# A 12-stage decoder on one core: hand-ordered mixture loop in layer 0, and a context LayerNorm in four steps

## Chip, cores and metric

One core of one Trainium2 chip runs the whole program. The metric is the device time of one execution in microseconds. Before the change it is 1590.72 us, the median of three runs.

## What is computed

A decoder of four layers, each with self-attention, cross-attention to a context and a feed-forward part, on 4 batches of 256 tokens with 128 features. Two pieces matter here: the cross-attention of layer 0 and the feed-forward part of layer 0.

```python
x = x + _L0_attn_ref(_layernorm(x), ...)
x = x + _L0_xattn_ref(_layernorm(x), ctx_1024, mask_BxS2_bk0, ...)
x = x + _L0_ffn_ref(_layernorm(x), L0_ffn_gate_w, shared..., routed...)   # 32 experts, the best one taken
...
def _L2_xattn_ref(features, masks, latents, gm, bm, ...):
    x = _layernorm(features, gm, bm)          # features = ctx_1024
    ...
```

In `_L0_ffn_ref` each of the 1024 tokens goes to one of 32 experts (hidden size 256), `silu(x @ gate) * (x @ up) @ down`, and a shared expert of the same form is added. The LayerNorm of the context, 4 x 512 rows, is needed in layer 2, but the kernel computes it while layer 0 runs.

## The kernel before

**Where the order of work comes from.** The program is written in Python order, and the framework then puts each engine's instructions into a fixed queue. Unless told otherwise it chooses that queue itself, in a simulated run made before the launch: when an engine is free in the simulation it takes, among the instructions whose inputs and buffers are ready, the one written first. An instruction written much later can so be pulled forward into a gap. [...] `tc.manual_schedule(engines=...)` makes the queues of the named engines follow the written order inside its block.

**The mixture loop (`mixture`, called from `ffn0`).** Tokens are sorted by expert into 16 blocks of 128 rows, each made of four groups of 32 rows (`per` = 32, `m` = 4); a group belongs to one expert. For block `b`:

- `fetch(b)`, L1053: GpSimd (POOL) gathers the 128 rows by an indirect DMA into `xb`, six buffers, five blocks ahead.
- `rows_T(b)`: PE turns `xb` (L1060) into a bank of tag `t`, and ACT copies it to `xbT` (L1062).
- `weights_in(b)`, L1034: DVE copies the four experts' first weights, 128x512 each, from the resident `e0h` to `wbh`, two buffers. The column offsets are read into DVE registers from the table `at`.
- `hidden(b)`: eight matmuls (L1075, two for each group of 32 rows), then ACT's Silu `sg` (L1173), then DVE's product `h` (L1174).
- `turned(b)`: PE turns `h` by two transposes (L1084) into a bank of tag `t`, and DVE copies it to `hT` (L1086).
- `weights_out(b)`, L1039: ACT copies the four experts' second weights, 128x256 each, from `e0d` to `wbd`, three buffers.
- `result(b)`: sixteen matmuls (L1096) into `y`; after every fourth block ACT copies `y` to `ys` (L1109) and SP's queue stores it to `done` (L1110).

The tag `t` has two PSUM banks, shared by `rows_T` and `turned`. An iteration of the loop (L1121 on) holds the steps of neighbouring blocks: `weights_in(b+1)`, `weights_out(b)`, `hidden(b)`, `rows_T(b+1)`, `fetch(b+5)`, `turned(b-1)`, `result(b-2)`. After the loop, layer 1 loads `w1x` through SP's queue and starts with matmuls on it (L1309). The same function serves layers 1 and 2 with `per` = 128; those have no weight copies.

**The context LayerNorm (`normalise_context`, L1984).** Layer 0's attention is woven by hand out of eight units, four for self-attention and then four for cross-attention; each unit has a list `beside` of extra steps, spread evenly over its length. A cross unit of batch `b` has two such steps, and each normalises two 128-row tiles of `cn` in place: `statistics` makes mean and variance on DVE (L287, L288) and the reciprocal root on POOL (L293, L295, the power -0.5); `scaled_by` then applies them on DVE (L301). POOL also computes the attention's own LayerNorm scaling (`xn`, L301) and adds a bias row to `x` (L347). DVE's main work in the units is the row maximum `mx` (L477), which reads PSUM banks of tag `s1` that PE fills.

Of the kernel before, what the change touches and what calls it, by code (L numbers as in the profile page):

```python
# [10 lines left out]

# [1 line left out]

# [1 line left out]

# [15 lines left out]
P = 128  # L33
# [3 lines left out]
NKT = SK // P  # L37
# [146 lines left out]
def decoder(ctx: ExitStack, tc: tile.TileContext, dr, out):  # L184
    nc = tc.nc
    V, A, G, T = nc.vector, nc.scalar, nc.gpsimd, nc.tensor
# [11 lines left out]
    def ps(tag):  # L198
        cols = 1024 if tag == "sc" else 512
        return psum[0].tile([P, cols], F32, tag=tag, name=tag, bufs=BANKS.get(tag, 2))  # L200

    @contextmanager
    def psum_pool(name):
        with tc.tile_pool(name=name, bufs=2, space=PSUM, reuse_waits="tile") as psum[0]:
            yield
# [19 lines left out]
    cn = const.tile([P, B * NKT, D], F32, tag="cn", name="cn")  # L225
# [49 lines left out]
    def normalise(srcs, dsts, on=None):  # L275

        scaled_by(statistics(srcs), srcs, dsts, on)

    def statistics(srcs, twice=False):

        n = len(srcs)
        mv = small.tile([P, 2, 2], F32, tag="mv", name="mv")
        for i, s in enumerate(srcs):
            st = small.tile([P, 6], F32, tag="st", name="st")
            V.bn_stats(st, s)  # L287
            V.bn_aggr(mv[:, i, :], st)  # L288
        ve = small.tile([P, 2], F32, tag="ve", name="ve")
        if twice:  # L290
            G.tensor_scalar(ve[:, :n], mv[:, :n, 1], 1.0 + EPS, EPS * EPS, ALU.mult, ALU.add)
        else:
            G.tensor_scalar(ve[:, :n], mv[:, :n, 1], EPS, None, ALU.add)  # L293
        rs = small.tile([P, 2], F32, tag="rs", name="rs")
        G.tensor_tensor(rs[:, :n], ve[:, :n], halves[:, :n], ALU.pow)  # L295
        return mv, rs

    def scaled_by(stats, srcs, dsts, on=None):
        mv, rs = stats
        for i, (s, d) in enumerate(zip(srcs, dsts)):  # L300
            (on or V).tensor_scalar(  # L301
                d, s, mv[:, i, 0:1], rs[:, i : i + 1], ALU.subtract, ALU.mult
            )
# [70 lines left out]
    def call(f, *args):  # L374
        return lambda *more: f(*args, *more)
# [362 lines left out]
    def turned(xn, pool):  # L738
        xnT = pool.tile([P, S], F32, tag="xnT", name="xnT", bufs=3)
        transposed(xn, xnT, tag="s1")  # L740
        return xnT
# [255 lines left out]
    def mixture(pool, n_e, per, hots, weights, rows_, wh, wd, activate, biases=None):  # L997
# [7 lines left out]
        m = P // per  # L1005
        size = -(-(k * NT * m + n_e - 1) // m)
        tiles_ = [slice(j * per, (j + 1) * per) for j in range(m)]
        n1, n2 = wh.shape[1] // n_e, wd.shape[1] // n_e
# [8 lines left out]
        xb, xbT, h, hT, y = {}, {}, {}, {}, {}  # L1017
        ahead = 5

        def offsets(i, b, engine):  # L1020

            _, values = nc.values_load_multi_w_load_instructions(
                at[0:1, b, i, :], engines=[engine], min_val=0, max_val=(n_e - 1) * widths[i],
                skip_runtime_bounds_check_because="an expert's number, limited to the last one's",
            )
            return values
# [3 lines left out]
        def weights_in(b):  # L1030

            w = wb[0, b] = pool.tile([P, m, n1], F32, tag="wbh", name="wbh", bufs=2)
            for j, v in enumerate(offsets(0, b, mybir.EngineType.DVE)):
                V.tensor_copy(w[:, j, :], wh[:, bass.ds(v, n1)])  # L1034

        def weights_out(b):
            w = wb[1, b] = pool.tile([P, m, n2], F32, tag="wbd", name="wbd", bufs=3)
            for j, v in enumerate(offsets(1, b, mybir.EngineType.Activation)):
                A.copy(w[:, j, :], wd[:, bass.ds(v, n2)])  # L1039

        def taken(i, b, n):

# [8 lines left out]
        def fetch(b):  # L1051
            xb[b] = pool.tile([P, D], F32, tag="xb", name="xb", bufs=ahead + 1)
            G.indirect_dma_start(  # L1053
                out=xb[b], out_offset=None, in_=sent[:, :],
                in_offset=bass.IndirectOffsetOnAxis(ap=token[:, b : b + 1], axis=0),
            )

        def rows_T(b):
            tp = ps("t")[:, :P]
            T.transpose(tp, xb[b], ident)  # L1060
            xbT[b] = pool.tile([P, P], F32, tag="xbT", name="xbT", bufs=3)
            A.copy(xbT[b], tp)  # L1062

        def hidden(b):
            o = [ps("g") for _ in range(0, n1, 512)]
            blocks = taken(0, b, 512)
            for i, p in enumerate(o):
                if biases is not None:
                    (at_h,) = offsets(0, b, mybir.EngineType.PE)
                    T.matmul(  # L1070
                        p, lhsT=onesb[0:3, :], rhs=biases[0:3, bass.ds(at_h, 512)],
                        start=True, stop=False,
                    )
                for r, w in blocks:
                    T.matmul(  # L1075
                        p[r], lhsT=xbT[b][:, r], rhs=w(512 * i), start=biases is None, stop=True,
                    )
            h[b] = pool.tile([P, n2], F32, tag="h", name="h", bufs=3)
            activate(pool, h[b], o)

        def turned(b):
            tp = ps("t")
            for i in range(nh):
                T.transpose(tp[:, i * P : (i + 1) * P], h[b][:, i * P : (i + 1) * P], ident)  # L1084
            hT[b] = pool.tile([P, n2], F32, tag="hT", name="hT", bufs=3)
            V.tensor_copy(hT[b], tp[:, :n2])  # L1086

        def result(b):
            g, i = b // 4, b % 4
            if i == 0:  # L1090
                y[g] = ps("y")
            cols = slice(i * P, (i + 1) * P)
            blocks = taken(1, b, P)
            for c in range(nh):
                for r, w in blocks:
                    T.matmul(  # L1096
                        y[g][r, cols], lhsT=hT[b][:, c * P : (c + 1) * P][:, r], rhs=w(c * P),
                        start=c == 0, stop=c == nh - 1 and biases is None,
                    )
            if biases is not None:  # L1100
                (at_b,) = offsets(2, b, mybir.EngineType.PE)
                T.matmul(
                    y[g][:, cols], lhsT=onesb[0:3, :],
                    rhs=biases[0:3, bass.ds(at_b + n_e * n1, P)], start=False, stop=True,
                )
            if b == groups[g][-1]:
                n = len(groups[g])
                ys = pool.tile([P, 4, D], F32, tag="ys", name="ys")
                A.copy(ys[:, :n, :], y[g][:, : n * P].rearrange("p (n d) -> p n d", n=n))  # L1109
                nc.sync.dma_start(  # L1110
                    done[4 * g * P : (4 * g + n) * P, :].rearrange("(n p) d -> p n d", p=P),
                    ys[:, :n, :],
                )
# [4 lines left out]
        if per < P:  # L1118
            weights_in(0)
        rows_T(0)  # L1120
        for b in range(size + 2):  # L1121
            if per < P and b + 1 < size:
                weights_in(b + 1)
            if per < P and b < size:
                weights_out(b)
            if b < size:
                hidden(b)
            if b + 1 < size:
                rows_T(b + 1)
            if b + ahead < size:  # L1130
                fetch(b + ahead)
            if 1 <= b <= size:
                turned(b - 1)
            if b >= 2:
                result(b - 2)

        def bring(b):
            out = []
# [842 lines left out]

    def normalise_context(b, i):  # L1984
        two = [cn[:, NKT * b + i, :], cn[:, NKT * b + i + 1, :]]
        normalise(two, two)

    def turn_context(b):
        tp = ps("s1")
# [16 lines left out]
    def layer_0(wh):  # L2006
        with ExitStack() as st:
            st.enter_context(psum_pool("ps0"))
            pool = attn_pool(st, "l0")
            neg0, neg0T = key_mask(pool, "mbk0", False)  # L2010
            for i in range(0, 32, 4):
                cols = slice(i * 512, (i + 4) * 512)
                nc.sync.dma_start(wh[:, cols], dr["e0h"][:, cols])
            units = self_units(pool, w0a, True, False, 0)
            units += cross_units(
                pool, w0x, 2, context_T,
                row_mask=lambda b: neg0[:, b * SK : (b + 1) * SK],
                key_bias=lambda b: lambda kt: neg0T[:, NKT * b + kt : NKT * b + kt + 1],
            )
            for u in units[B:]:  # L2020
                u.beside = [call(normalise_context, u.b, i) for i in range(0, NKT, 2)]
            woven(pool, units, SK)

    def layer_1(w, loads):
# [38 lines left out]
    with tc.tile_pool(name="e1", bufs=1, reuse_waits="tile") as experts:  # L2063
        w1x = load("w1x", pool=late, on=nc.sync)

        def loads():
# [6 lines left out]
        ahead = right.enter_context(  # L2073
            tc.tile_pool(name="ahead", bufs=1, side="right", reuse_waits="tile")
        )
# [27 lines left out]
```

## Time and profile before

| what | value |
|---|---|
| median of three runs | 1590.72 us (1585.98 to 1591.83) |
| profiled execution, own time | 1587.75 us |
| its span, first to last instruction | 1586.0 us |
| PE busy | 1351.7 us (85%) |
| DVE / ACT / POOL busy | 824.2 / 726.2 / 277.9 us |
| mean granted TensorE clock | 0.916 |
| layer 0's attention | to about 288 us |
| routing and shared expert of layer 0 | about 288 to 316 us |
| mixture loop of layer 0 | 316.2 to 366.5 us |

The last three rows come from the timeline. The profiled execution lies 0.2% under the median, inside the spread of the runs. In timeline lines the columns are start, length, engine, line, operation, output and input, count, and in brackets how long the engine had been idle and what ended it; PEld is the loading of a matmul's weights. A group of instructions on one line is shown with its joint length.

### The profile page before, as it was taken

How to read it: one execution, taken by the hardware profiler on the slowest of the kernel's cores; microseconds unless marked ns; L12 is line 12 of the kernel's file. 1: busy time of each engine (PE TensorE's matmuls, PEld its weight loads, DVE VectorE, ACT ScalarE, POOL GpSimd, SP SyncE). 2: the span in 40 equal slices, each digit the busy share in tenths (PEclk: the TensorE clock that was granted, in tenths of full speed). 3: DMA queues.
4: the chain of work that ended last, by engine and by line, in shares of the span. 5: the costliest groups of instructions: out<-in, count | busy, mean ns of one | idle time of the engine just before them, and what ended most of it. 6: DMA issues, size and time to landing. Idle time of an engine off the chain costs nothing.

```text
span 1586.0 us, 26992 instructions
## 1 busy us (share of the span) xinstructions
PE 1351.7 (85%) x10188; PEld 699.6 (44%) x10189; DVE 824.2 (52%) x2723; ACT 726.2 (46%) x1440; POOL 277.9 (18%) x401
## 2 busy tenths in 40 slices
PE   5997998776777998889999999999595699999963
PEld 3542333424345564544555554455363344333322
DVE  5676663475665336654443453351433556765336
ACT  0552666365642334367667656665021044344431
POOL 5223110134011415100000000000333522211000
PEclk9997999797997999999999999999697599999985
DMA  8000000311052215220111000000322000000000
GB/s 318 1 1 1 2 1 2 119 41 34 1 205 71 63 33 197 87 100 14 54 41 41 1 1 1 1 1 1 138 42 62 14 2 1 1 2 1 1 2 12
DMA packets 34980, 67.97 MB, mean 43 GB/s; under 512 B 5014, under 2 KB 18752, under 8 KB 32928
## 3 DMA queue, kind: packets, MB, share of 16 engines
q1 hardware_dynamic: 30434, 49.88, 9.0%
q0 software_dynamic: 3264, 6.69, 1.9%
q10 hardware_dynamic: 1152, 9.67, 1.5%
q8 instruction: 82, 1.34, 0.4%
q14 instruction: 48, 0.39, 0.1%
HBM read 49.55 MB, written 16.68 MB: 42 GB/s over the span
## 4 chain that ended last, share of the span: by engine, by line
PE 69%; DVE 11%; ACT 7%; POOL 5%; issue 5%; DMA 2%; ACTq 0%; SPq 0%; POOLq 0%; DVEq 0%
PE o L571 7%; PE s L535 7%; PE s L470 6%; PE o L1830 6%; PE s L1810 5%; PE g L1075 5%; PE f L1759 4%; PE s L522 3%; PE y L1096 2%; PE f L1745 2%; PE s L529 2%; PE f L1715 2%; PE s L1803 2%; PE s L343 2%; POOL back L1143 2%
## 5 line engine op out<-in xcount | busy, mean ns | idle before, releaser
L470 PE MATMUL s<-kc,qm 32*128 32x256 f32 (+1 forms) x1024 | 222.1, 574 | 13.9 <-POOL qm L425 8.4
L552 ACT ACTIVATE pr<-s 128x512 f32<-128x512 f32 x256 | 137.9, 596 | 193.4 <-PE s L535 183.1
L535 PE MATMUL s<-qm,kc 32*128 32x512 f32 (+1 forms) x896 | 209.0, 609 | 0.0
L477 DVE TENSOR_REDUCE mx<-s 128x1 f32<-128x512 f32 (+1 forms) x192 | 122.6, 685 | 68.7 <-PE s L535 52.0
L1770 ACT ACTIVATE ss<-ss,ntop 128x768 f32<-128x768 f32 x128 | 118.8, 929 | 85.6 <-DVE ntop L1768 85.2
L571 PE MATMUL o<-pr,v 128*32 128x256 f32 (+1 forms) x1792 | 144.8, 389 | 9.0 <-ACT os L577 4.1
L293 POOL TENSOR_SCALAR ve<-mv 128x2 f32<-128x2 f32 (+1 forms) x56 | 12.7, 227 | 767.9 <-DVE mv L288 703.5
L1764 DVE CUSTOM_DVE_ANT_0 ss<-f,n 128x512 f32<-128x512 f32 x128 | 83.4, 689 | 75.4 <-PE f L1759 75.4
L470 PEld LDWEIGHTS s<-kc,qm 32*128 32x128 f32 x1024 | 89.7, 210 | 69.7 <-issue 19.3
L481 DVE CUSTOM_DVE_ANT_0 junk<-s,nmif 128x512 bf16<-128x512 f32 x128 | 83.0, 688 | 54.0 <-PE s L470 53.7
L1830 PE MATMUL o<-pr,v 128*64 128x256 f32 x768 | 109.5, 397 | 0.0
L554 ACT ACTIVATE pr<-s,n 128x512 f32<-128x512 f32 x128 | 80.1, 690 | 59.9 <-PE s L535 39.6
L1810 PE MATMUL s<-qT,kT 64*128 64x256 f32 x768 | 103.1, 384 | 0.0
L571 PEld LDWEIGHTS o<-pr,v 128*32 128x32 f32 x1792 | 40.2, 109 | 118.3 <-issue 89.5
L1817 ACT ACTIVATE pr<-s,n 128x512 f32<-128x512 f32 x128 | 80.2, 679 | 20.8 <-PE s L1810 20.6
L529 PE MATMUL s<-mT,selg 12*128 12x256 bf16 x768 | 80.9, 277 | 8.4 <-DVE mx L477 6.1
L425 POOL TENSOR_SCALAR qm<-q,consts 128x256 f32<-128x256 f32 x64 | 58.6, 932 | 158.1 <-ACT q L422 127.7
L1053 POOL DMA_INDIRECT xb<-sent,token x62 | 60.5, 976 | 125.2 <-PE t L1060 68.6
L1752 DVE CUSTOM_DVE_ANT_0 ss<-f,nought 128x256 f32<-128x256 f32 x128 | 46.8, 421 | 60.2 <-PE f L1745 60.1
L1759 PE MATMUL f<-kT,qT 64*128 64x512 f32 x256 | 76.2, 624 | 0.1
L1830 PEld LDWEIGHTS o<-pr,v 128*64 128x64 f32 x768 | 48.2, 137 | 60.6 <-issue 24.0
L1810 PEld LDWEIGHTS s<-qT,kT 64*128 64x128 f32 x768 | 68.2, 192 | 6.2 <-issue 0.2
(405 smaller groups left out, 2401.3 us busy)
## 6 DMA issues: line engine op xcount, KB each, us to landing
e0h<-in_e0h SPq DMA_DIRECT2D x8, 1024.0 KB
kd<-ahead SPq DMA_DIRECT2D x20, 256.0 KB
vd<-ahead SPq DMA_DIRECT2D x20, 256.0 KB
kT<-kd SPq DMA_DIRECT2D x20, 256.0 KB
v<-vd SPq DMA_DIRECT2D x5, 1024.0 KB
e0d<-in_e0d SPq DMA_DIRECT2D x1, 4096.0 KB
e1h<-in_e1h ACTq DMA_DIRECT2D x1, 4096.0 KB
done<-ys SPq DMA_DIRECT2D x14, 256.0 KB
```

The costliest lines, as they stand in the source:

```text
L470: T.matmul(sc[:, i, :], lhsT=u.qm[r, g + i, qt * P : (qt + 1) * P], rhs=u.kc[r, :], start=u.row_mask is None, stop=True,)
L477: V.tensor_reduce(u.mx[:, qt, j, g : g + per], sc, AX.X, ALU.max)
L481: V.tensor_tensor_reduce(junk[:, : u.nk], sc[:, i, :], u.rows_mask(qt), 1.0, -3e38, ALU.add, ALU.max, accum_out=u.mx[:, qt, j, g + i : g + ...
L529: T.matmul(sc[:, i, :], lhsT=selg[r, gp + i, :], rhs=u.mT[r, :], start=u.cols_mask is None and i == 0, stop=False,)
L535: T.matmul(sc, lhsT=u.kc[r, kt * P : (kt + 1) * P], rhs=u.qm[r, gp : gp + 2, first:], start=u.clip, stop=True,)
L552: A.activation(dst, sc, AF.Exp)
L571: T.matmul(u.po[gp][32 * j : 32 * j + 32, i, first:], lhsT=u.v[:, kt, 4 * j + gp + i, :], rhs=u.pr[gp, kt, j][:, i, first:], start=kt + i ...
L1759: T.matmul(sc[h], lhsT=qT[u, c][hrow[h], qt * P : (qt + 1) * P], rhs=kT[u, c][hrow[h], :SK], start=True, stop=True,)
L1764: V.tensor_tensor_reduce(ss[qt][h][:, :SK], sc[h], neg1[:, b * SK : (b + 1) * SK], 1.0, -3e38, ALU.add, ALU.max, accum_out=mx[:, qt, h, 1:2],)
L1770: A.activation(ss[qt][h], ss[qt][h], AF.Exp, bias=ntop[:, qt, h, c : c + 1], accum_out=total[:, qt, h, c : c + 1],)
L1810: T.matmul(sc[h][:, i, :], lhsT=kT[u, c][hrow[h], kt * P : (kt + 1) * P], rhs=qT[u, c][hrow[h], :], start=False, stop=i == 1,)
L1830: T.matmul(po[u, g][hrow[h], i, :], lhsT=v[u][:, kt, n * hd : (n + 1) * hd], rhs=pr[u, g, kt, h][:, i, :], start=kt + i == 0, stop=kt + i ...
```

## The change

Five edits:

1. In layer 0's mixture, DVE, ACT and PE follow the written order (POOL and SP stay with the scheduler).
2. `weights_out(b)` stands later in the iteration: behind `turned(b-1)`, ahead of `result(b-2)`.
3. The fourth of each block's second-weight copies goes from ACT to POOL, which reads its own offsets.
4. The copy of `hT` goes from DVE to ACT (only with `per` = 32).
5. `normalise_context` becomes four steps of a unit, first both statistics and then both scalings, so that a scaling stands half a unit behind its statistics.

```diff
         def weights_out(b):
             w = wb[1, b] = pool.tile([P, m, n2], F32, tag="wbd", name="wbd", bufs=3)
+            on_pool = offsets(1, b, mybir.EngineType.Pool)
             for j, v in enumerate(offsets(1, b, mybir.EngineType.Activation)):
-                A.copy(w[:, j, :], wd[:, bass.ds(v, n2)])
+                if j < m - 1:
+                    A.copy(w[:, j, :], wd[:, bass.ds(v, n2)])
+                else:
+                    G.tensor_copy(w[:, j, :], wd[:, bass.ds(on_pool[j], n2)])
...
             hT[b] = pool.tile([P, n2], F32, tag="hT", name="hT", bufs=3)
-            V.tensor_copy(hT[b], tp[:, :n2])
+            if per < P:
+                A.copy(hT[b], tp[:, :n2])
+            else:
+                V.tensor_copy(hT[b], tp[:, :n2])
...
-        for b in range(size + 2):
-            if per < P and b + 1 < size:
-                weights_in(b + 1)
-            if per < P and b < size:
-                weights_out(b)
-            if b < size:
-                hidden(b)
...
+        by_hand = {mybir.EngineType.DVE, mybir.EngineType.Activation, mybir.EngineType.PE}
+        with tc.manual_schedule(engines=by_hand) if per < P else nullcontext():
+            for b in range(size + 2):
+                if per < P and b + 1 < size:
+                    weights_in(b + 1)
+                if b < size:
+                    hidden(b)
+                if b + 1 < size:
+                    rows_T(b + 1)
+                if b + ahead < size:
+                    fetch(b + ahead)
+                if 1 <= b <= size:
+                    turned(b - 1)
+                if per < P and b < size:
+                    weights_out(b)
+                if b >= 2:
+                    result(b - 2)
...
-    def normalise_context(b, i):
-        two = [cn[:, NKT * b + i, :], cn[:, NKT * b + i + 1, :]]
-        normalise(two, two)
+    def normalise_context(b):
+        twos = [[cn[:, NKT * b + j, :] for j in (i, i + 1)] for i in range(0, NKT, 2)]
+        stats = {}
+        def first(i):
+            stats[i] = statistics(twos[i])
+        def then(i):
+            scaled_by(stats[i], twos[i], twos[i])
+        return [call(f, i) for f in (first, then) for i in range(len(twos))]
...
-                u.beside = [call(normalise_context, u.b, i) for i in range(0, NKT, 2)]
+                u.beside = normalise_context(u.b)
```

More of the change, by code (lines that the diff above doesn't have):

```diff
@@ L14 @@
-from contextlib import ExitStack, contextmanager
+from contextlib import nullcontext, ExitStack, contextmanager
 import numpy as np
@@ L1120, in mixture @@
         rows_T(0)
-        for b in range(size + 2):
-            if per < P and b + 1 < size:
-                weights_in(b + 1)
-            if per < P and b < size:
-                weights_out(b)
-            if b < size:
-                hidden(b)
[L1128 to L1135, printed above, removed]
+        by_hand = {mybir.EngineType.DVE, mybir.EngineType.Activation, mybir.EngineType.PE}
[15 more added lines that the diff above has]
+                    result(b - 2)
         def bring(b):
```

## The prediction

> **What bounds the kernel now.** I read the page first: PE is busy 85% of the span and heads the chain of waits, but that is an average. The change touches two stretches, so I read those alone: the waits and the timeline of 316.2 to 366.5 us (the mixture loop) and of 112 to 160 us (the context LayerNorm). In the loop no engine is full: from 334.5 to 358.5 us PE and DVE are each busy 20.4 and ACT 17.5 of 24 us. The waits of that window show a ring (waiter, what it waited for, total us, times, longest):
>
> ```profile
> DVE h L1174 <- ACT sg L1173: 12.2, 11, 2.7
> ...
> PEld t L1084 <- ACT xbT L1062: 7.7, 5, 1.7
> ...
> ACT wbd L1039 <- PE y L1096: 5.9, 6, 1.2
> ```
>
> One turn of it in the timeline:
>
> ```profile
> 353.50 0.64 PE L1096 MATMUL y<-wbd,hT 128*32 128x128 f32 x16
> ...
> 354.26 1.33 ACT L1039 COPY wbd<-e0d 128x256 f32 x4 [1.19 <-PE y L1096]
> 354.33 1.07 PE L1075 MATMUL g<-wbh,xbT 128*32 128x512 f32 x8
> 355.50 0.26 ACT L1062 COPY xbT<-t 128x128 f32<-128x128 f32 x1
> 355.65 0.38 ACT L1173 ACTIVATE sg<-g 128x256 f32<-128x256 f32 x1
> ...
> 355.81 0.44 PE L1084 MATMUL t<-consts,h 128*128 128x128 f32 x2 [0.41 <-ACT xbT L1062]
> ...
> 356.18 0.65 PE L1096 MATMUL y<-wbd,hT 128*32 128x128 f32 x16
> ```
>
> ACT's four `wbd` copies wait for the `y` matmuls to free a buffer; behind them in ACT's queue stands the `xbT` copy; PE's next transposes wait for it; behind those stand the next `y` matmuls. The turn takes 2.68 us, and so does the mean: `y` starts at 332.45 and 361.95 with 11 blocks between, 29.5 / 11 = 2.68. Elsewhere PE runs through without a stall:
>
> ```profile
> 348.06 0.64 PE L1096 MATMUL y<-wbd,hT 128*32 128x128 f32 x16
> ...
> 348.63 0.33 PE L1060 MATMUL t<-consts,xb 128*128 128x128 f32 x1
> ...
> 348.89 1.07 PE L1075 MATMUL g<-wbh,xbT 128*32 128x512 f32 x8
> ...
> 349.89 0.44 PE L1084 MATMUL t<-consts,h 128*128 128x128 f32 x2
> 350.25 0.38 PEld L1096 LDWEIGHTS y<-wbd,hT 128*32 128x32 f32 x16 [0.17 <-issue]
> ```
>
> 350.25 - 348.06 = 2.19 us is PE's own work for a block: 0.57 + 0.26 + 1.00 + 0.36.
>
> In the LayerNorm stretch DVE stops for POOL, PE then runs out of PSUM, and its clock drops:
>
> ```profile
> 123.67 0.60 DVE L301 TENSOR_SCALAR cn<-cn,mv,rs 128x128 f32<-128x128 f32 x2 [3.75 <-POOL rs L295]
> ...
> 125.91 0.37 PE L529 MATMUL s<-mT,selg 12*128 12x256 bf16 x1 [5.34 <-DVE mx L477]
> ```
>
> The same happens at 150.08 us (3.72 us on DVE, 4.74 on PE). All sixteen scalings together waited 8.6 us, in four waits.
>
> [...] The trace agrees that meeting costs time, but shows POOL paying: an `xn` of 0.80 us took 1.13 at 1224.55 and a `qm` of 0.925 took 1.35, each across a DVE SBUF-to-SBUF operation of 0.73 to 0.76 us; the loop's gathers took 0.95 alone and up to 1.15 beside `wbh` copies, whose foursome stayed at 1.42 to 1.58. [...] `g`'s eight matmuls take 1.93 us at 321 and 1.06 later; after both LayerNorm stops they run slow until about 132 and 159 us.
>
> **The loop, part by part.** Order on PE becomes g(b), R(b+1) (the transpose of `xb`), T(b-1) (of `h`), y(b-2). With g(b) starting at 0 the tight stretch gives R at 1.00, T at 1.26, y at 1.62, the next g at 2.19.
> - ACT per block: Silu 0.28, `xbT` 0.16, `hT` 0.27 (starts one after another in the trace; a 128x256 copy from PSUM lasts 0.37), three `wbd` of 0.31, a quarter of `ys` 0.48: 0.28 + 0.16 + 0.27 + 0.93 + 0.12 = 1.76. Silu starts at 1.21, `xbT` at 1.49 and ends at 1.75, ahead of the next g at 2.19. `wbd` begins at about 2.1 and needs y(b-3), which is over since 0.07; the ring is cut, since nothing that PE needs soon stands behind it. Register reads (at most the 0.19 seen before a `wbd`) fit the 0.4 us left.
> - DVE per block: four `wbh` 1.43 and `h` 0.34 = 1.77, where it had 2.1 with `hT`. `h` is needed one iteration later.
> - PSUM: R and T follow each other with both `t` banks free, so each can have its own. Were they given one bank, T would wait for `xbT` at 1.75 and the old 2.68 would be back.
> - POOL: no f32 copy of this shape is in the trace. Low bound: the 128-element cast L1258 takes 0.285 and a near-empty memset 0.10, so 0.10 + 256 x 1.45 ns = 0.47; [...] High bound: `qm` of that shape, 0.92, plus 0.35 for meeting a DVE copy. I take 0.6, and 0.3 for four register reads (the issue gap between gathers is 0.30). Eleven gathers of 0.95 + 0.30 and sixteen copies: 13.8 + 16 x 0.9 = 28 us from about 323 on, done near 351; a copy has two iterations until y needs it. At the high bound 13.8 + 16 x 1.57 = 39 us, to 362, and POOL would set the end.
> - SP: `w1x` stood behind the third `ys` store (issued at 360.59). It moves left with that store, to about 355; PE needs it at 359, a cover of 4 us that was 5.6 before. If it went behind the last store, that would take back about 3 us.
>
> So PE is the bound at 2.19 us. The start: g(0) no longer stands behind R(1), which waited for a gather (320.60); it can start at 319.95 instead of 320.98. With the cold durations of the trace the first blocks give g at 322.6, 325.6, 328.5, 331.0, 333.3, and then ten blocks of 2.19 bring g(15) to 355.2 (before: 362.4). Behind it T(14), y(13), Silu, `h`, T(15), y(14), `hT`, y(15): about 3.8 us, end 359.0 instead of 366.5. **Gain 7.5 us**; bounds 9 and, with `t` on one bank or POOL at its high bound, 0 to 3.5. What follows (L1309, the `kbd` copies, the last store and its gathers) hangs on the loop's end and moves with it.
>
> **The LayerNorm steps.** The bn, scaling and POOL instructions are the same in number; their written place moves, the statistics of a unit's halves from 0.25 and 0.75 of it to 0.125 and 0.375, the scalings to 0.625 and 0.875. But the trace shows them far from their written place: the first scalings run at 124 us, before their unit begins (about 145: the `cT` copies at 160.7 and 198.1 stand 0.41 into units of 37 us), those of the third and fourth cross unit at 161 and 199, straight behind the `cT` copies that free them. They are pulled into gaps that the planner sees on DVE, where everything written earlier isn't ready yet; later placing doesn't change that choice. What changes: a first statistic (0.125) now ranks ahead of the `x` addition L347 (0.2475 of a unit) on POOL, which took 0.86 us in between, and DVE's aggregation for the second half no longer ranks behind the first scaling. At 124 us the last scaling still waits for the same POOL queue; at 150 it comes 0.9 us sooner. **Gain 0.9 us**; bounds: 15 us if both stops go (5.34 + 4.74 idle and some 5 at half clock), and a loss of 5 (one more such stop).
>
> **Sum.** 7.5 + 0.9 = 8.4 us: the profiled execution's 1587.75 becomes 1579.4. It lies 3.0 under the median; against that, 1590.72 - 8.4 = 1582.3, and I say 1582. A measurement can tell about 0.5%, 8 us, from no change, so this likeliest case sits on that edge.
>
> **Rivals.**
> - *The LayerNorm stops go too* (0.26): the written place decides after all, and `mx` runs ahead of the scalings. For it: `mx` was ready near 119.2, before any scaling could be. Another 10 to 14 us: 1568 to 1572.
> - *The loop gains half* (0.15): POOL's copies or a shared `t` bank keep the period at 2.4 to 2.6: 1586 to 1590.
> - *Nothing moves* (0.05): the planner had already the written order where it matters, 1590. Against it: the ring.
> - [...] DVE's 1.77 plus a copy of 0.92 is 2.69, the old period: that is the point from which it decides. [...] A part of this case ends within 0.5%. Against it: the foursome of 1.42 to 1.58 beside gathers.
>
> The likeliest case has 0.44, some 0.6 of it beyond 0.5%. Faster: 0.26 + 0.26 = 0.52. Within: 0.18 + 0.15 + 0.05 + 0.03 = 0.41. Slower: 0.07. The range runs from the middle of the first rival to the edge of no change, 1569 to 1592.
>
> **What would show it.** In the new timeline: `y` 2.2 us apart; `wbd` without "PE y" as releaser; `wbh` foursomes still under 1.6; POOL copies of 0.5 to 0.8; loop end near 359; `w1x` issued before the last store; two waits of `cn` for `rs` over 2.5 us still there. Periods of 2.6, POOL copies over 1 us, or no such `cn` waits would prove me wrong.

## The result, and the profile after

Two measurements, each beside the kernel before on the same chip:

| kernel | median | before beside it | ratio, 95% interval |
|---|---|---|---|
| changed, first time | 1582.0 us (1577.2 to 1585.5, 11 runs) | 1591.1 us | 0.9943 [0.9928, 0.9957] |
| changed, second time | 1579.8 us (1576.1 to 1582.1, 8 runs) | 1585.3 us | 0.9962 [0.9948, 0.9975] |

The first is a gain of 9.1 us, the second of 6.0; forecast were 8.4 and a time of 1582. The two intervals overlap only from 0.9948 to 0.9957. The second agrees with what the parts below add up to, 0.9965, and the first does not; why is open. The profiled execution of the changed kernel took 1585.5 us (span 1583.7), the slowest of its eleven, so the two spans (1586.0 before) hide most of the gain, and stretches have to be compared.

**The mixture loop.** From the first gather to the end of the last `y` it took 42.3 us (318.92 to 361.20), where it had taken 50.3. In the eight profiles of kernels whose loop is this one or close to it (the changed kernel twice, and a1, a3, b2, c2, c3 and c4 below) the figure is 39.7 to 42.3; in the two with the old loop it is 47.9 and 50.3. In the new code lines have moved on by 2 to 9: `wbd` is L1041 on ACT and L1043 on POOL, `xb`'s transpose L1064, `xbT` L1066, `g` L1079, `h`'s transposes L1088, `hT` L1091, `y` L1103, `sg` L1182, `h` L1183. The waits of 316 to 362 us (waiter, what it waited for, total us, times, longest):

```profile
POOL wbd L1043 <- PE y L1103: 6.1, 4, 1.7
PEld g L1079 <- ACT xbT L1066: 3.0, 6, 0.7
DVE h L1183 <- ACT sg L1182: 3.0, 4, 1.4
...
DVE bg L1314 <- DMA w1x<-in_w1x: 2.1, 1, 2.1
```

Now no transpose waits for `xbT` and no `wbd` copy on ACT for `y`; once the loop runs, the largest wait for another engine is POOL's, 6.1 us for a `y` that frees its buffer, and no `y` is seen waiting for POOL. One turn on PE, late in the loop:

```profile
352.11 0.33 PE L1064 MATMUL t<-consts,xb 128*128 128x128 f32 x1
352.27 0.38 PE L1088 MATMUL t<-consts,h 128*128 128x128 f32 x2
352.58 0.64 PE L1103 MATMUL y<-wbd,hT 128*32 128x128 f32 x16
353.05 1.04 PE L1079 MATMUL g<-wbh,xbT 128*32 128x512 f32 x8
354.02 0.33 PE L1064 MATMUL t<-consts,xb 128*128 128x128 f32 x1
```

354.02 - 352.11 = 1.91 us without a stall (the view shows idle time from 0.15 us on): 0.16 from R (`xb`) to T (`h`), 0.31 to `y`, 0.47 to `g`, 0.97 to the next R. The same turn on ACT:

```profile
352.32 0.38 ACT L1182 ACTIVATE sg<-g 128x256 f32<-128x256 f32 x1
352.60 0.26 ACT L1066 COPY xbT<-t 128x128 f32<-128x128 f32 x1
352.75 0.39 ACT L1091 COPY hT<-t 128x256 f32<-128x256 f32 x1
353.26 1.02 ACT L1041 COPY wbd<-e0d 128x256 f32 x3
```

The next `sg` starts at 354.23, again 1.91 later, and no idle time stands in brackets. That ACT had a little room all the same, `b2_act4` below shows. DVE keeps the same pace: from this foursome of `wbh` copies to the next, at 353.26, are 1.91 us, and a POOL copy lies inside it:

```profile
351.35 1.63 DVE L1034 COPY wbh<-e0h 128x512 f32 x4
352.91 0.41 DVE L1183 TENSOR_TENSOR h<-sg,g 128x256 f32<-128x256 f32 x1
```

```profile
351.51 0.53 POOL L1043 COPY wbd<-e0d 128x256 f32 x1 [1.74 <-PE y L1103]
```

The foursome lasts 1.63 us here. From the third on, the foursomes of this loop took 1.50 to 2.15 us, the longest with two POOL copies and parts of two gathers beside them; they lasted 1.42 to 1.58 before.

**The LayerNorm.** Both stops are still there, one of 3.62 us on DVE (5.21 on PE) at 125, the other at about 150. The waits of 112 to 160 us:

```profile
DVE cn L301 <- POOL rs L295: 7.9, 4, 3.6
```

That is 0.7 us less than the 8.6 of before.

### The profile page after: what moved, and what is told of

Its sections match the earlier page's. It is cut to its first block, busy times and chain, and to the rows that moved or that the text cites. A ratio compares the mean times of both kernels' runs of the same rounds, so it can differ in the third digit from the quotient of the medians.

```text
span 1583.7 us, 27050 instructions
## 1 busy us (share of the span) xinstructions
PE 1354.8 (86%) x10188; PEld 703.7 (44%) x10189; DVE 823.2 (52%) x2707; ACT 726.1 (46%) x1440; POOL 285.2 (18%) x417
## 4 chain that ended last, share of the span: by engine, by line
PE 71%; DVE 12%; ACT 6%; issue 5%; POOL 4%; DMA 1%; ACTq 0%; DVEq 0%; POOLq 0%; SPq 0%
PE s L535 7%; PE o L571 7%; PE s L470 6%; PE o L1839 6%; PE g L1079 5%; PE s L1819 5%; PE f L1768 4%; PE s L522 3%; PE y L1103 2%; PE f L1754 2%; PE s L529 2%; PE f L1724 2%; PE s L343 2%; PE s L1812 2%; DVE mx L477 1%
```

## The experiments

A ratio is always to the kernel before, run beside it. "Loop" is the time from the first gather to the end of the last `y`, "period" the mean distance of the `g` groups from the fifth to the fifteenth block (2.63 before, 2.04 after, 2.06 in the repeat), both from one profiled execution.

### The two halves of the change, and the whole again

`a1_loop_only` has the four loop edits and the old LayerNorm, `a2_ln_only` the LayerNorm edit alone, `b1_after_again` is the changed kernel once more.

> The four edits of the mixture loop, with the context LayerNorm in its old two steps. My theory: nearly the whole gain is the loop's, so 7 to 8 us faster than before (the loop 316 to 361 shortened by 8). Rival, the LayerNorm carries half of it: only 4 us faster.

> The LayerNorm in four steps alone, with the old loop. My theory: the scalings stay where the planner pulled them to, one of two stops gets 0.9 us shorter; 0.5 to 1 us faster, not to be told from no change, two waits of cn for rs over 2.5 us still there. Rival, the written place decides: both stops gone, 10 us or more faster.

> The changed kernel once more, beside the runs below on one chip. If its parts add up (loop alone 0.9966, LayerNorm alone 0.9999), its ratio lies at 0.9965. If the two together bring more than their sum, it repeats 0.9943.

| kernel | ratio, 95% interval | loop, us | period, us | `cn` waits for `rs` |
|---|---|---|---|---|
| a1_loop_only | 0.9966 [0.9949, 0.9982] | 41.5 | 2.06 | 8.6 |
| a2_ln_only | 0.9999 [0.9987, 1.0011] | 47.9 | 2.64 | 7.9 |
| b1_after_again | 0.9962 [0.9948, 0.9975] | 41.5 | 2.06 | |

The gain is the loop's. The LayerNorm edit takes 0.7 us off its waits, too little for its ratio to show. The parts add up: 0.9966 x 0.9999 = 0.9965.

### The scalings held at their written place

Does the written place of the scalings matter, once they really stay there?

```diff
-    def scaled_by(stats, srcs, dsts, on=None):
+    def scaled_by(stats, srcs, dsts, on=None, pin=False):
...
-            (on or V).tensor_scalar(
+            ins = (on or V).tensor_scalar(
...
+            if pin:
+                tc.keep_in_program_order(ins)
...
-            scaled_by(stats[i], twos[i], twos[i])
+            scaled_by(stats[i], twos[i], twos[i], pin=True)
```

> The changed kernel, and each scaling of the context held on DVE's queue behind the instruction written before it (issue order only), so that it can't be pulled ahead. My theory of the stops: both waits of DVE for POOL go, PE's idle 5.3 and 4.7 us go, and so does most of the half clock after them: 10 to 14 us faster than the changed kernel, 1568 to 1572. Rival: the scalings and statistics cost DVE the same time where PE is already the bound, and late statistics hold other LayerNorms up through the four buffers: 0 to 4 us faster only.

Measured: 0.9912 [0.9892, 0.9931]; its wait of `cn` for `rs` is 0.7 us in all. Set against the 0.9965 that the parts of the changed kernel give on the same chip this is 0.9947, or 8.4 us, below the 10 to 14 expected. `c4_pinned_act4` (further down) holds the scalings too. Where they run, in the answers for the tile `cn` of the changed kernel and of c4 (count, min/median/max ns, first and last start):

```profile
L301 DVE TENSOR_SCALAR cn<-cn,mv,rs x16: 337/341/346, 125.1 to 200.5; 128x128 f32<-128x128 f32 x16
```

```profile
L301 DVE TENSOR_SCALAR cn<-cn,mv,rs x16: 316/342/530, 154.6 to 238.8; 128x128 f32<-128x128 f32 x16
```

What that is worth, in the table by stretches: the length, the busy time of PE, PEld, DVE, ACT and POOL with the number of instructions, then the granted clock. The changed kernel, then c4:

```profile
112.00:160.00 48.00, 36.20 (x294) 14.16 (x294) 31.75 (x98) 14.71 (x26) 17.54 (x32) 0.87 0.00 1
```

```profile
112.00:160.00 48.00, 44.41 (x435) 18.43 (x436) 37.19 (x101) 23.47 (x40) 17.77 (x30) 1.00 0.00 1
```

In the same 48 us PE does 435 matmul instructions instead of 294, and the granted clock is 1.00 instead of 0.87 (in a3, with the same edit, 418 and 0.96). PE's longest idle time there is 1.47 us. So the planner's pulling forward, not the place in the text, made the stops. Behind the two stops of 5.2 and 4.2 us in the changed kernel the granted clock was 0.50 from 127.3 to 133 us and, in the mean, 0.51 from 154 to 161; in the kernel before, behind 5.34 and 4.74 us, it was 0.50 from 125.9 to 132 and from 153 to 159. The traces show no more of its cause than that. In a3 and c4 the loop begins at 305 us, in the other twelve profiles between 312 and 319. Most of these distances are larger than the gain by the ratios; where the rest goes stays open.

### The order alone

`a4_auto_order` is the changed kernel without the manual order:

```diff
-        with tc.manual_schedule(engines=by_hand) if per < P else nullcontext():
+        with nullcontext():
             for b in range(size + 2):
```

> The changed kernel without the written order: DVE, ACT and PE of the loop are left to the scheduler, while the copies stay where the change puts them (one on POOL, hT on ACT). My theory: spreading the copies is worth about half; the ring of ACT and PE comes back in part since xbT again stands behind wbd copies. Period 2.3 to 2.5, 3 to 5 us slower than the changed kernel. Rival 1, the order is all: 8 us slower. Rival 2, the copies are all: no difference.

Measured: 0.9977 [0.9964, 0.9990], loop 45.1, period 2.39. By the loop's length about half of the gain needs the written order; the ratio alone can't be told from a1's 0.9966 on the same chip. The ring that the expectation names is not back: from 330 to 354 us no transpose waits for `xbT`. What differs is PE's queue. The planner puts the transposes of `h` into the midst of the `y` matmuls and that of `xb` behind them: in one turn `h`'s start at 338.38, six of `y` at 338.74, `xb`'s at 339.09, `g` at 339.35, ten of `y` at 340.23 and the next transposes of `h` at 340.76, with no idle time on PE in brackets. That this order is what costs the 0.3 to 0.5 us (2.39 against the changed kernel's 2.04 and its 1.91 late in the loop) is an estimate, not shown by this run; `b4_rows_first` below tests a plainer case of it.

### The fourth copy back on ACT

```diff
-            on_pool = offsets(1, b, mybir.EngineType.Pool)
+            on_pool = None
             for j, v in enumerate(offsets(1, b, mybir.EngineType.Activation)):
-                if j < m - 1:
+                if j < m:
                     A.copy(w[:, j, :], wd[:, bass.ds(v, n2)])
                 else:
```

> The changed kernel with all four second-weight copies on ACT, none on POOL. Theory, ACT is one of three engines level at 1.91 us for a block: ACT gets 0.31 more, 2.2 us; but DVE's wbh foursome falls back from 1.5 to 1.85 to 1.43, as no POOL copy meets it. The loop takes 41 to 42 us instead of 40, the kernel 1 to 2 us longer. [...] Rival, the ring returns: period 2.6, 7 us longer.

Measured: 0.9951 [0.9937, 0.9966], loop 41.8, period 2.05. No gain from the copy on POOL can be seen: of the changed kernel's two ratios one is lower and one higher. DVE without it:

```profile
348.46 1.44 DVE L1034 COPY wbh<-e0h 128x512 f32 x4
...
350.39 1.43 DVE L1034 COPY wbh<-e0h 128x512 f32 x4
```

Late in the loop, where no gather runs any more, the foursomes are back at 1.43 to 1.44, against 1.50 to 1.65 at that place in the changed kernel; so POOL's copies lengthened them there. Earlier, beside gathers, they took up to 1.71 in b2 too. ACT did not need the 2.2 us expected: from the fifth block on most turns took 1.91 to 1.98 us, so it had had room for a fourth copy, and only each fourth turn, with the copy `ys`, took 2.42 to 2.46. In the changed kernel those with `ys` were shorter, 2.14 to 2.22, and most others longer, 1.91 to 2.22. It seems that what the POOL copy spares ACT where `ys` stands is paid on DVE elsewhere; the periods are alike, 2.04 to 2.06 and 2.05.

### hT back on DVE, and what it turned up

```diff
-            if per < P:
+            if False:
                 A.copy(hT[b], tp[:, :n2])
             else:
                 V.tensor_copy(hT[b], tp[:, :n2])
```

> The changed kernel with the copy of hT back on DVE. DVE then has 1.63 + 0.28 + 0.34 = 2.25 us for a block, ACT 1.6. If DVE is the bound, the period is 2.25 and the loop 3 to 5 us longer. If PE at 1.91 sets it alone and DVE has slack, under 1 us longer.

Measured: 0.9994 [0.9983, 1.0005], loop 46.0, period 2.70, in steady turns 2.61. Nearly all is lost, more than DVE's load explains. PE's turn (`y` is L1103, T L1088):

```profile
347.93 0.33 PE L1064 MATMUL t<-consts,xb 128*128 128x128 f32 x1
348.74 0.44 PE L1088 MATMUL t<-consts,h 128*128 128x128 f32 x2 [0.48 <-ACT xbT L1066]
349.11 0.64 PE L1103 MATMUL y<-wbd,hT 128*32 128x128 f32 x16
```

T turns `h`; it reads nothing of `xbT`. Yet it waits for ACT's `xbT` copy, as in the kernel before. The only thing that they can share is the PSUM tile of tag `t` that `xbT` reads, and the memory addresses in the built programs show it: the bank of each R and of the T behind it, from the second pair on.

```
before   R0 T0, R1 T0, R1 T1, R0 T0, R1 T0, R1 T1, R0 T0, R1 T0, R1 T0, R1 T1, R0 T0, R1 T1, R0 T0
after    R0 T1 throughout
b3       R0 T1 twice, then R0 T0, R1 T1, R0 T0, R1 T1 ... to the end
```

In 9 of 13 pairs of the kernel before (the expectation of c1 below counts 8) R and T stand in one bank, so T can't start until ACT has emptied it. The trace of before bears it out. Numbering those pairs in order, T starts 1.25 to 1.26 us after R in the pairs 5, 8 and 9, which have two banks, and 1.58 to 2.16 us after it in 3, 4, 6, 7 and 10 to 13, which have one; the first two, in the slow start of the loop, wait for other things too. From one T to the next, these three turns took 2.2 us and the others from the third pair on 2.6 to 3.3. So a new theory: **the shared bank closes the ring, not the place of the `wbd` copies.** Three kernels tested it. In c1 and c2, T has a bank of its own, taken from `g`, which keeps three; c3 has separate banks already, and puts the copies back to where they stood:

```diff
-BANKS = {"s1": 7, "o1": 1, "f": 3, "s": 4, "o": 1, "g": 4}
+BANKS = {"tt": 1, "s1": 7, "o1": 1, "f": 3, "s": 4, "o": 1, "g": 4}
...
-        return psum[0].tile([P, cols], F32, tag=tag, name=tag, bufs=BANKS.get(tag, 2))
+        n = 3 if tag == "g" and own_bank[0] else BANKS.get(tag, 2)
+        return psum[0].tile([P, cols], F32, tag=tag, name=tag, bufs=n)
...
         def turned(b):
-            tp = ps("t")
+            tp = ps("tt" if per < P else "t")
```

```diff
                 if per < P and b + 1 < size:
                     weights_in(b + 1)
+                if per < P and b < size:
+                    weights_out(b)
...
-                if per < P and b < size:
-                    weights_out(b)
                 if b >= 2:
                     result(b - 2)
```

> The kernel before, with one change: the transposes of h (T) get a PSUM bank of their own (taken from tag g, four banks to three), so that T never stands in the bank of the transpose of xb (R). In the kernel before, R and the T behind it were given the same bank in 8 of 13 full turns, and in those T waits until ACT has copied xbT. Theory A (the shared bank is the link that closes the ring): PE no longer waits for xbT between R and T; period 2.2 to 2.4 us, loop 3 to 6 us shorter than 48 to 50, ratio to before 0.996 to 0.998. Theory B (the place of the wbd copies in ACT's queue is what holds the loop; xbT is late for whoever reads it, and g reads it as well): the period stays at 2.6 to 2.7 and the ratio at 0.999 to 1.001.

> The changed kernel with hT's copy on DVE as before (as b3_hT_dve) and, new, a PSUM bank of its own for T. In b3_hT_dve R and T shared a bank from the fifth block on, and the period was 2.61. Theory A (b3 lost the gain to the shared bank): the period falls to DVE's own sum, 2.1 to 2.3 us, loop 42 to 43.5, ratio 0.9965 to 0.998. Theory B (DVE's load and the order in its queue, wbh behind hT, were the loss): 2.5 to 2.65, ratio 0.999 to 1.000.

> The changed kernel with weights_out back at its old place ahead of hidden, in the written order; R and T keep separate banks. Theory A (the banks decide): the copies wait for a y that is nearly over and fill the time in which ACT would wait for g; period 1.95 to 2.1, ratio 0.994 to 0.997, as the changed kernel. Theory B (the ring of the prediction: wbd copies ahead of xbT in ACT's queue wait for y, and PE waits for xbT): period 2.4 to 2.7, ratio 0.999 to 1.000.

| kernel | ratio, 95% interval | loop, us | period, us |
|---|---|---|---|
| c1_before_own_bank: before, T with its own bank | 0.9972 [0.9960, 0.9984] | 44.4 | 2.20 |
| b3_hT_dve: changed, `hT` on DVE | 0.9994 [0.9983, 1.0005] | 46.0 | 2.70 |
| c2_hT_dve_own_bank: b3, T with its own bank | 0.9948 [0.9933, 0.9963] | 41.0 | 2.32 |
| c3_copies_first: changed, copies at their old place | 0.9967 [0.9954, 0.9979] | 40.4 | 2.15 |

Theory A holds in all three, with sizes a little off: c2 gained more than expected, and c3's period (2.15) was a little over the 2.1. In c1 nothing of the change is made but the bank, and half to three quarters of the gain is there, by the two ratios of the changed kernel. A turn of it (`g` is L1078, T L1087, `y` L1099, R L1063):

```profile
344.90 0.44 PE L1087 MATMUL tt<-consts,h 128*128 128x128 f32 x2
345.27 0.64 PE L1099 MATMUL y<-wbd,hT 128*32 128x128 f32 x16
345.84 0.33 PE L1063 MATMUL t<-consts,xb 128*128 128x128 f32 x1
346.10 1.07 PE L1078 MATMUL g<-wbh,xbT 128*32 128x512 f32 x8
347.10 0.44 PE L1087 MATMUL tt<-consts,h 128*128 128x128 f32 x2
```

```profile
343.83 1.32 ACT L1042 COPY wbd<-e0d 128x256 f32 x4 [0.38 <-PE y L1099]
345.11 0.39 ACT L1176 ACTIVATE sg<-g 128x256 f32<-128x256 f32 x1
345.39 0.26 ACT L1065 COPY xbT<-t 128x128 f32<-128x128 f32 x1
```

2.20 us on PE, without a wait, where the kernel before needed 2.68. ACT's four `wbd` copies still wait for `y` and still stand ahead of `xbT`, as before; T just doesn't wait for `xbT` any more. In c2 nothing but the bank is changed against b3, and the loss is gone; `hT` on DVE then costs what DVE's sum says, with the period at 2.02 late in the loop:

```profile
344.99 1.44 DVE L1037 COPY wbh<-e0h 128x512 f32 x4
346.35 0.41 DVE L1186 TENSOR_TENSOR h<-sg,g 128x256 f32<-128x256 f32 x1
346.68 0.41 DVE L1096 COPY hT<-tt 128x256 f32<-128x256 f32 x1
347.01 1.42 DVE L1037 COPY wbh<-e0h 128x512 f32 x4
```

The POOL copies of these turns start at 344.74 and 346.75, take 0.41 and 0.40 us, and fall for the most part beside `hT`'s copy, which reads PSUM; here they lengthen neither it (0.41 us, 0.42 in the kernel before) nor the foursomes (1.44 and 1.42).

In c3 ACT's three `wbd` copies stand ahead of Silu and `xbT` again, and the loop is as short as the changed kernel's.

Why the framework gave T the bank of R when `hT` was on DVE was not looked into. By the addresses, R and T have banks 0 and 1 throughout in all the built programs where ACT copies `hT` and one tag serves both: the changed kernel, a1, a3, b2, b4, c3, c4 and also a4, whose order is the planner's. They share in some or most turns in those where DVE copies it: before, a2 and b3. So it was edit 4, which the prediction counts only as work moved from DVE to ACT, that parted the banks.

### The order of the transposes

`b4_rows_first` has separate banks and the written order, but R ahead of `g`, as before the change, instead of next to T:

```diff
+                if b + 1 < size:
+                    rows_T(b + 1)
                 if b < size:
                     hidden(b)
-                if b + 1 < size:
-                    rows_T(b + 1)
```

> The changed kernel with the transpose of the next block's rows ahead of the hidden matmuls in each iteration (the order of before on PE), all else the same. My prediction took 2.19 us as PE's own work, and the changed kernel shows 1.91. If the order on PE makes that difference (two transposes side by side start 0.16 apart, a transpose between y and g costs 0.37), the period returns to 2.2 and the loop is 3 to 4 us longer. If the 2.19 held a hidden wait for other engines, the period stays under 2.0 and nothing changes.

```profile
348.00 0.44 PE L1088 MATMUL t<-consts,h 128*128 128x128 f32 x2
348.38 0.64 PE L1103 MATMUL y<-wbd,hT 128*32 128x128 f32 x16
348.95 0.33 PE L1064 MATMUL t<-consts,xb 128*128 128x128 f32 x1
349.21 1.07 PE L1079 MATMUL g<-wbh,xbT 128*32 128x512 f32 x8
```

Its turn is 2.19 to 2.20 us (the T of the turn before starts at 345.81) against 1.91, with no stall in either, and its period 2.29, where b1 had 2.06. So the 2.19 held no hidden wait; c1, too, runs at 2.20 in that order. Its ratio is 0.9993 [0.9982, 1.0003]. Against the 0.9962 of b1 on the same chip that is 4.9 us, and 15 blocks of 0.29 are 4.4. But its profiled loop, 42.6, is only 1.1 us longer than b1's 41.5: its first five turns took 11.5 us in place of 12.8, and b1's turns were not all as short as 1.91. Why the ratio lost more than the profiled loop, and why c1 with a loop of 44.4 has the better ratio, stays open.

### The best version

`c4_pinned_act4` is the changed kernel with the scalings held in place and all four copies on ACT.

> Candidate for the best version: the changed kernel with the scalings of the context LayerNorm held at their written place (as a3_ln_pinned) and all four wbd copies on ACT (as b2_act4). If the two edits are independent: ratio 0.989 to 0.993, both LayerNorm stops gone (cn waits below 1 us), loop 40.5 to 42, wbh foursomes 1.43 to 1.49. Rival: a3's 0.9912 was helped by a favourable run; then 0.993 to 0.996.

Measured: 0.9896 [0.9878, 0.9914], 1569.5 us beside 1586.2 of the kernel before, the fastest of all. Against b2, which differs by the holding alone, 0.9896 / 0.9951 = 0.9945, 8.7 us. The loop took 39.7, the foursomes 1.43 to 1.49 in most blocks. The two edits add up, as far as intervals of this width can tell.

## Why the prediction was right, and where not

The time and the shares of its two parts were right; one reason behind the larger part was not, and with another it had luck. Of the five edits, two can be seen in the runs: the written order (a4, b4) and `hT` on ACT (b3, with c1 and c2), which parted the banks. The later `wbd` (c3), the copy on POOL (b2) and the LayerNorm in four steps (a2) changed no ratio that shows.

- **The ring.** The chain was read rightly from the timeline (R had ended at 354.40, and `xbT`, next on ACT, started at 355.50, straight behind the four `wbd` copies), but not its link from `xbT` to T. The prediction put it so: "the ring is cut, since nothing that PE needs soon stands behind it", from moving `wbd`. c3 shows that the place of the copies doesn't matter, b3 that moving them doesn't help with a shared bank, c1 that separate banks help without moving them. The prediction's line on PSUM ("Were they given one bank, T would wait for `xbT` at 1.75 and the old 2.68 would be back") had the true cause as a side condition: b3 gave 2.61. It took the kernel before's stall for a queue's fault, though T has no use for `xbT`. The tight turn that it quoted (348.06 and on) was a pair with two banks. That each would have its own was expected because both follow each other "with both `t` banks free". That is no sufficient reason: b3 has the same order, and they share. They were apart because of `hT`'s move, which it counted only as work moved from DVE to ACT; this was luck. Its list of waits is that of the whole loop: from 334.5 to 358.5 us `h` waited only 2.6 of those 12.2 us for `sg`.
- **PE's own work.** 2.19 us was taken from the kernel before. The change brings R next to T, and the turn is 0.47 + 0.97 + 0.16 + 0.31 = 1.91. This term was mis-sized by 0.28, because a step's price was held to be the same in another order; b4 shows it at 2.20 in the old one.
- **DVE.** 1.43 + 0.34 = 1.77 was too low: beside POOL's copies the foursomes took 1.50 to 2.15. "`wbh` foursomes still under 1.6" was wrong. The prediction had taken POOL to be the one that pays where the two meet, from the trace of before. In this loop DVE pays: late in it, with no gather beside, 1.43 without the POOL copies (b2) and 1.63 with one of 0.53 us inside. The rival in which the kernel gets slower (0.10) has POOL's work lengthen DVE's copies; that was real, at some 0.3 us for a block on average where 0.92 would have decided.
- **Why the sum held all the same.** Two errors pull against each other: PE's 0.28 us less per block, and DVE's copies that were longer, one reason why the turns took 2.07 and not 1.91. Of the first five blocks it forecast 13.35 us (measured 13.72), then ten blocks of 2.19 (measured 20.72 / 10 = 2.07), a tail of 3.8 (measured 4.03), and a start sooner by 1.03 (measured 0.93). In all 42.8 us from the first gather to the end, measured 42.3; the gain over the two profiles with the old loop is 5.6 to 8.0 us.
- **POOL.** Sixteen copies of 0.39 to 0.65 us, median 0.49, where 0.6 was taken. Late in the loop they wait for `y` (6.1 us in four waits), not for time on POOL. That they gain nothing (b2) the prediction did not say.
- **`w1x`.** Issued at 357.12, ahead of the last store (361.88), as forecast (about 355). The cover of 4 us was just used up: DVE waited 2.10 us, PE 0.23.
- **The LayerNorm steps.** 0.9 us forecast, 0.7 measured; both stops remained, for the reason given, that the planner pulls the scalings out of their written place. The rival that they go had 10 to 14 us; a3 and c4 show 8 to 9.

## What to carry to other kernels

When an instruction waits for an engine whose result it doesn't read, look for the buffer that both use: with two PSUM banks under one tag, the framework may put a tile into the bank just being emptied (9 of 13 pairs of the kernel before), and a bank of its own then freed this loop with its copies left where they stood. A price read in one order of matmuls need not hold in another (1.91 and 2.19 us a block here); read it again with its neighbours. And a step that a planner pulls forward has to be held in place before its place in the text means anything.

## What the runs showed of the hardware

- PE: the transposes of `xb` and `h` side by side, rather than apart among the 32-row matmuls, saved 0.28 us a block (1.91 against 2.19 to 2.20) at the same instructions. R and T cost 0.16 + 0.31 us as neighbours, where R alone cost 0.26 and T 0.36 to 0.37 before; `y` cost 0.47 with `g` behind it and 0.57 with R behind it.
- DVE and POOL: a 128x256 f32 copy from SBUF to SBUF took POOL 0.39 to 0.65 us. With no gather beside, it brought DVE's foursome of 128x512 copies from 1.43 us (b2) to 1.50 to 1.65 (changed kernel). Beside a DVE copy from PSUM it lengthened nothing (c2: 0.40 and 0.41 us, foursomes 1.42 to 1.44). With gathers beside and no POOL copy, foursomes took up to 1.71 (b2).
- PE idle for 5.2 and 4.2 us: holding the scalings, which removed both, was worth 8 to 9 us; granted clock in the 48 us around them 0.87 against 0.96 and 1.00, and right behind each 0.50 and 0.51.
